# A graph layer on one core: edges on two column halves, carried sums and a row table in place of accumulating scatters

## The chip, the cores and the metric

The kernel runs on one core of one Trainium2 chip. The metric is the device time of one launch in microseconds (us); the time before is the median of six runs, 5170.73 us (5166.9 to 5174.27). A profile of one further execution goes with it.

## What is computed

One layer over 10000 nodes of 512 features and 160000 edges, all in float32. With xn = layernorm(x):

```python
h   = xn @ W
agg = segment_sum(h[src] * edge_weight[:, None], dst, 10000)   # dst is sorted
x   = x + relu(agg + bias) + mix(xn)        # mix: linear attention of 8 heads, then a norm
x   = x + ffn(layernorm(x))                 # 6 experts, one weighted mixture for all nodes
```

The kernel sums the gathered rows of xn first and multiplies by W afterwards, which is the same sum. `dst` is drawn so that low nodes have many edges and high nodes about eight.

## The kernel before

Rows are worked on in 20 chunks of 512 nodes (the last 272), four sub-rows a partition. Five stages follow one another.

**A** (lines 150 to 158): a chunk is loaded, normalised on VectorE with a power on GpSimd (lines 122 to 130, 126), and stored to `xn_d`. At the same time ten stores (line 209) fill the 10240 rows of `acc_d` with zeros.

**B** (lines 251 to 294): for each chunk transposes, the key product `pk`, exp, transposes and the context product `pc`. **C** (lines 297 to 365): for each chunk the query product `pq`, softmax, transposes, the output product `po` and a norm.

The **edges** are worked off during B and C. They lie in 1250 tiles of 128 edges, in order of `dst`. Six tiles (BATCH) make a step, 209 steps in all. For each tile an indirect DMA issued by GpSimd gathers 128 rows of `xn_d` into a buffer `msg` (line 217; a pool of 3 x BATCH = 18 buffers). VectorE makes a mask `sel` for the step (lines 221 and 224): for each edge a row of 128 columns (WIN) with its weight in the column of its node, counted from the step's first node. TensorE adds up the six products mask x rows in one PSUM tile of 128 nodes (line 229), ScalarE copies it out (line 231), and an indirect DMA with addition scatters its 128 rows into `acc_d` (line 232). Neighbouring steps can share nodes, so the scatters follow one another.

Lines 372 to 417 count the edges outside their step's 128 nodes; only if there are any does a loop over all tiles work them off one at a time.

**D** (lines 439 to 457): chunks of `acc_d` are loaded by SyncE's queue (line 441), transposed, multiplied by W, and the layer's first half is finished; GpSimd keeps a running sum `xsum` (line 457). **E** (from line 553): the feed-forward part, 256 products of 128x512 a chunk in two groups (lines 567 and 576).

Each engine works through its own list in order. A planner makes these lists from its own estimate of durations, so the order on an engine is not that of the text: pieces of a step's products stand between the products of B and C, 1 to 6 at a time in B and up to 31 in a row in C. The calls that spread the edges over B and C are these:

```python
for c, (_, r) in enumerate(chunks):
    edges_until((c - LEAD) / (2 * NCH - LEAD))          # B, line 254
...
    edges_until((NCH + c - LEAD) / (2 * NCH - LEAD))    # C, line 330
```

Of the kernel before, what the change touches and what calls it, by code (L numbers as in the profile page):

```python
# [8 lines left out]
F32 = mybir.dt.float32  # L9
I32 = mybir.dt.int32  # L10
AF = mybir.ActivationFunctionType
ALU = mybir.AluOpType
AX = mybir.AxisListType
# [3 lines left out]
P = 128  # L17
SUB = 4
EPS = 1e-5
HEAD = 64  # L20
QSCALE = HEAD ** -0.5
BATCH = 6
WIN = 128
PARTITIONS_OF_6 = [
    (6,), (5, 1), (4, 2), (4, 1, 1), (3, 3), (3, 2, 1), (3, 1, 1, 1),
    (2, 2, 2), (2, 2, 1, 1), (2, 1, 1, 1, 1), (1, 1, 1, 1, 1, 1),
# [4 lines left out]
def gps_layer_kernel(  # L31
# [19 lines left out]
    nc = tc.nc  # L51
    N, D = x.shape
    NET = src.shape[1]
# [18 lines left out]
    def tokens(t, c):  # L72
        b, r = chunks[c]
        return t[b : b + r * SUB, :].rearrange("(p s) d -> p s d", s=SUB)
# [14 lines left out]
    iota_w = const.tile([P, WIN], F32, name="iota_w")  # L89
    nc.gpsimd.iota(iota_w, pattern=[[1, WIN]], base=0, channel_multiplier=0,  # L90
                   allow_small_or_imprecise_dtypes=True)
    pid = const.tile([P, 1], F32, name="pid")
    nc.gpsimd.iota(pid, pattern=[[0, 1]], base=0, channel_multiplier=1,
                   allow_small_or_imprecise_dtypes=True)

    earlier = const.tile([P, P], F32, name="earlier")
# [7 lines left out]
    nc.scalar.dma_start(bias_b, gnn_bias.to_broadcast([P, D]))  # L104
    gamma_b = const.tile([P, D], F32, name="gamma_b")
    nc.scalar.dma_start(gamma_b, gamma.to_broadcast([P, D]))
    stats2 = const.tile([P, NCH, SUB, 2], F32, name="stats2")


# [2 lines left out]
    y_d = [dram.tile([r, SUB, D], F32, name=f"y_d{c}") for c, (_, r) in enumerate(chunks)]  # L112
    x1_d = [dram.tile([r, SUB, D], F32, name=f"x1_d{c}") for c, (_, r) in enumerate(chunks)]

    ACC_ROWS = -(-(N + P) // (8 * P)) * 8 * P
    acc_d = dram.tile([ACC_ROWS, D], F32, name="acc_d")

    def row_stats(t, r, mv):

# [41 lines left out]
    with ExitStack() as ph:  # L161
# [16 lines left out]
        nc.sync.dma_start(wq, w_qkv_t[:, :D].rearrange("(k p) d -> p k d", p=P))  # L178
        wo = wp.tile([P, KB, D], F32, name="wo")
        nc.sync.dma_start(wo, w_out_t.rearrange("(k p) d -> p k d", p=P))  # L180
        NB = -(-NET // BATCH)
        full = NET // BATCH
        base = ep.tile([P, NB], F32, name="base")
        idx = ep.tile([P, NB], I32, name="idx")
        place = ep.tile([P, NET], F32, name="place")
        tmp_ctx = ph.enter_context(ExitStack())
        tmp = tmp_ctx.enter_context(tc.tile_pool(name="edge_t", bufs=1))
        row_sb = tmp.tile([P, NET], I32, name="row_sb")
        nc.sync.dma_start(row_sb, dst[0:1, :].to_broadcast([P, NET]))

        nc.vector.tensor_copy(base[:, :full], row_sb[:, : full * BATCH].rearrange(
            "p (b j) -> p b j", j=BATCH)[:, :, 0])
        if NB > full:
            nc.vector.tensor_copy(base[:, full:], row_sb[:, full * BATCH : full * BATCH + 1])
        tmp_ctx.close()
        nc.vector.tensor_scalar(idx, base, pid, None, op0=ALU.add)

        nc.vector.tensor_copy(place, dst_sb)
        nc.vector.tensor_tensor(
            place[:, : full * BATCH].rearrange("p (b j) -> p b j", j=BATCH),  # L200
            place[:, : full * BATCH].rearrange("p (b j) -> p b j", j=BATCH),
            base[:, :full, None].to_broadcast([P, full, BATCH]), ALU.subtract)
        if NB > full:
            nc.vector.tensor_scalar(place[:, full * BATCH :], place[:, full * BATCH :],
                                    base[:, full : full + 1], None, op0=ALU.subtract)

        view = acc_d.rearrange("(b p) d -> p b d", p=P)
        for b in range(0, ACC_ROWS // P, 8):
            nc.scalar.dma_start(view[:, b : b + 8, :], zero[:, None, :].to_broadcast([P, 8, D]))

        def edges(b):

            t0 = b * BATCH
            n = min(BATCH, NET - t0)
            m = [mp.tile([P, D], F32, name="msg") for _ in range(n)]
            for j in range(n):
                nc.gpsimd.indirect_dma_start(  # L217
                    out=m[j], out_offset=None, in_=xn_d,
                    in_offset=bass.IndirectOffsetOnAxis(ap=src_sb[:, t0 + j : t0 + j + 1], axis=0))
            sel = ew.tile([P, BATCH, WIN], F32, name="sel")  # L220
            nc.vector.tensor_tensor(  # L221
                sel[:, :n, :], iota_w[:, None, :].to_broadcast([P, n, WIN]),
                place[:, t0 : t0 + n, None].to_broadcast([P, n, WIN]), ALU.is_equal)
            nc.vector.tensor_tensor(  # L224
                sel[:, :n, :], sel[:, :n, :],
                w_sb[:, t0 : t0 + n, None].to_broadcast([P, n, WIN]), ALU.mult)
            pm = psum_e.tile([P, D], F32, name="pm")
            for j in range(n):
                nc.tensor.matmul(pm, sel[:, j, :], m[j], start=j == 0, stop=j == n - 1)  # L229
            part = ew.tile([P, D], F32, name="part")  # L230
            nc.scalar.copy(part, pm)  # L231
            nc.gpsimd.indirect_dma_start(  # L232
                out=acc_d, out_offset=bass.IndirectOffsetOnAxis(ap=idx[:, b : b + 1], axis=0),
                in_=part, in_offset=None, compute_op=ALU.add)

        done = [0]

        def edges_until(share):
            stop = NB if share >= 1 else int(NB * share)
            while done[0] < stop:  # L240
                edges(done[0])
                done[0] += 1
# [54 lines left out]
        with ExitStack() as pb:  # L297
# [30 lines left out]
            for c, (_, r) in enumerate(chunks):  # L328
# [31 lines left out]
                for s in range(SUB):  # L360
# [2 lines left out]
                    nc.vector.scalar_tensor_tensor(ot[:r, s, :], ot[:r, s, :], mv[:r, s, 1:2],  # L363
                                                   xt[:r, s, :], op0=ALU.mult, op1=ALU.add)
                nc.sync.dma_start(y_d[c], ot[:r])
            edges_until(1)

        with ExitStack() as pb:  # L370
            fp = pb.enter_context(tc.tile_pool(name="far", bufs=1))
            inside = fp.tile([P, NET], F32, name="inside")
            nc.vector.tensor_scalar(inside, place, 0.0, None, op0=ALU.is_ge)
            w_far = fp.tile([P, NET], F32, name="w_far")
            nc.vector.scalar_tensor_tensor(w_far, place, float(WIN), inside, op0=ALU.is_lt, op1=ALU.mult)
            n_in = fp.tile([P, 1], F32, name="n_in")
            nc.vector.tensor_reduce(n_in, w_far, axis=AX.X, op=ALU.add)
            nc.vector.tensor_scalar(w_far, w_far, 0.0, None, op0=ALU.is_equal)
            nc.vector.tensor_tensor(w_far, w_far, w_sb, ALU.mult)
            pn = psum.tile([1, 1], F32, name="pn", tag="ps")  # L380
            nc.tensor.matmul(pn, n_in, ones, start=True, stop=True)
            n_far = fp.tile([1, 1], I32, name="n_far")
            nc.vector.tensor_scalar(n_far, pn, -1.0, float(NET * P), op0=ALU.mult, op1=ALU.add)
            any_far = nc.values_load(n_far[0:1, 0:1], min_val=0, max_val=NET * P)
            with tc.If(any_far > 0):
                with tc.For_i(0, NET) as t:
                    cs = fp.tile([P, 1], I32, name="cs")
                    nc.vector.tensor_copy(cs, src_sb[:, bass.ds(t, 1)])
                    cd = fp.tile([P, 1], F32, name="cd")
                    nc.vector.tensor_copy(cd, dst_sb[:, bass.ds(t, 1)])  # L390
                    cw = fp.tile([P, 1], F32, name="cw")
                    nc.vector.tensor_copy(cw, w_far[:, bass.ds(t, 1)])
                    m = fp.tile([P, D], F32, name="m_far")
                    nc.gpsimd.indirect_dma_start(
                        out=m, out_offset=None, in_=xn_d,
# [10 lines left out]
                    off = fp.tile([P, 1], F32, name="off")  # L406
                    nc.vector.tensor_scalar(off, cd, spare, None, op0=ALU.subtract)
                    nc.vector.scalar_tensor_tensor(off, seen, 0.0, off, op0=ALU.is_equal, op1=ALU.mult)
                    to = fp.tile([P, 1], I32, name="to")
                    nc.vector.tensor_scalar(to, off, spare, None, op0=ALU.add)  # L410
                    pm = psum.tile([P, D], F32, name="pm_far", tag="ps")
                    nc.tensor.matmul(pm, sel, m, start=True, stop=True)
                    part = fp.tile([P, D], F32, name="part_far")
                    nc.vector.tensor_copy(part, pm)
                    nc.gpsimd.indirect_dma_start(
                        out=acc_d, out_offset=bass.IndirectOffsetOnAxis(ap=to, axis=0),
                        in_=part, in_offset=None, compute_op=ALU.add)


# [16 lines left out]
    with ExitStack() as ph:  # L436
        io = ph.enter_context(tc.tile_pool(name="d_io", bufs=2))
        psum = ph.enter_context(tc.tile_pool(name="d_ps", bufs=3, space=PSUM))
        for c, (_, r) in enumerate(chunks):
            at = io.tile([P, SUB, D], F32, name="at")  # L440
            nc.sync.dma_start(at[:r], tokens(acc_d, c))
            yt = io.tile([P, SUB, D], F32, name="yt")
            nc.sync.dma_start(yt[:r], y_d[c])
            aT = io.tile([P, KB, SUB * P], F32, name="aT")
            transposed(aT, at, r, psum, "pt")
            gt = io.tile([P, SUB, D], F32, name="gt")
            for s in range(SUB):
                po = psum.tile([P, D], F32, name="po")
                times(po, aT, s, r, wg)
                nc.vector.tensor_tensor(gt[:r, s, :], po[:r, :], bias_b[:r], ALU.add)  # L450
            nc.vector.scalar_tensor_tensor(yt[:r], gt[:r], 0.0, yt[:r], op0=ALU.max, op1=ALU.add)
            nc.scalar.dma_start(x1_d[c], yt[:r])
            mv = stats2[:, c]
            row_stats(yt, r, mv)
            xn = io.tile([P, SUB, D], F32, name="xn")
            normalize(xn, yt, r, mv)
            nc.gpsimd.tensor_tensor(xsum[:r], xsum[:r], xn[:r], ALU.add)  # L457
# [164 lines left out]
```

## Time and profile before

| what | us |
|---|---|
| median of six runs | 5170.73 |
| the profiled execution | 5162.64 |
| its span | 5160.9 |
| stage A, until the first product | 0 to 176 |
| stages B and C, with the edges | 176 to 2557 |
| gap, until the first transposes of D | 2557 to 2582 |
| stage D | 2582 to 2913 |
| stage E | 2913 to 5161 |

PE (TensorE) is busy 4867.9 us of the span, DVE (VectorE) 1474.3, ACT (ScalarE) 627.5, POOL (GpSimd) 1897.7. A float32 matrix product is two records in the profile, each with its own weight load (PEld). The records of PE overlap, so the pace is read from start to start or from the length of a group in the chain, not from the mean length of a record. Stretches are us from the span's start.

### The profile page before, as it was taken

How to read it: one execution, taken by the hardware profiler on the slowest of the kernel's cores; microseconds unless marked ns; L12 is line 12 of the kernel's file. 1: busy time of each engine (PE TensorE's matmuls, PEld its weight loads, DVE VectorE, ACT ScalarE, POOL GpSimd, SP SyncE). 2: the span in 40 equal slices, each digit the busy share in tenths (PEclk: the TensorE clock that was granted, in tenths of full speed). 3: DMA queues.
4: the chain of work that ended last, by engine and by line, in shares of the span. 5: the costliest groups of instructions: out<-in, count | busy, mean ns of one | idle time of the engine just before them, and what ended most of it. 6: DMA issues, size and time to landing. Idle time of an engine off the chain costs nothing. (4 is left out here: it accounts for less than half of the span.)

```text
span 5160.9 us, 33449 instructions
## 1 busy us (share of the span) xinstructions
PE 4867.9 (94%) x12542; PEld 2220.1 (43%) x12542; DVE 1474.3 (29%) x2527; ACT 627.5 (12%) x1135; POOL 1897.7 (37%) x1613
## 2 busy tenths in 40 slices
PE   0699999999999999999799899999999999999999
PEld 0344444444444444444344344444444444444444
DVE  6333333333555555455466500000000000000000
ACT  0111111111111111111100111001111000111100
POOL 1544677777677777777633300000000000000000
PEclk9999999999999999999899999999999999999999
DMA  9855777777777777777675200000000000000000
GB/s 409 287 159 158 198 204 203 207 204 188 232 213 216 215 216 218 214 221 197 160 263 202 95 17 17 17 17 29 20 17 17 17 17 17 33 17 17 13 9 13
DMA packets 181719, 668.21 MB, mean 129 GB/s; under 512 B 28296, under 2 KB 29320, under 8 KB 151692
## 3 DMA queue, kind: packets, MB, share of 16 engines
q0 software_dynamic: 130096, 382.56, 28.6%
q1 hardware_dynamic: 28416, 192.13, 9.8%
q10 hardware_dynamic: 23044, 91.36, 4.4%
q8 instruction: 99, 1.62, 0.1%
q14 instruction: 64, 0.52, 0.0%
HBM read 487.79 MB, written 178.16 MB: 129 GB/s over the span
## 5 line engine op out<-in xcount | busy, mean ns | idle before, releaser
L217 POOL DMA_INDIRECT msg<-xn_d,src_sb x1250 | 1290.5, 1032 | 671.2 <-PE pm L229 329.1
L229 PE MATMUL pm<-msg,sel 128*128 128x512 f32 x2500 | 1132.8, 597 | 225.3 <-DMA msg<-xn_d,src_sb 222.7
L576 PE MATMUL po<-w_sb,hf 128*128 128x512 f32 (+2 forms) x2560 | 1102.3, 592 | 0.0
L567 PE MATMUL ph<-xnT,w_sb 128*128 128x512 f32 (+2 forms) x2560 | 1079.6, 583 | 0.0
L229 PEld LDWEIGHTS pm<-msg,sel 128*128 128x128 f32 x2500 | 460.7, 191 | 779.2 <-issue 664.8
L561 POOL TENSOR_TENSOR xt<-xt,b_b 128x2048 f32<-128x2048 f32 (+1 forms) x20 | 90.0, 4504 | 1857.3 <-DVE xn L130 1827.6
L576 PEld LDWEIGHTS po<-w_sb,hf 128*128 128x128 f32 (+2 forms) x2560 | 480.3, 188 | 618.3 <-issue 618.2
L567 PEld LDWEIGHTS ph<-xnT,w_sb 128*128 128x128 f32 (+1 forms) x2560 | 485.3, 190 | 578.5 <-issue 573.3
L578 DVE TENSOR_TENSOR xt<-xt,po 128x512 f32<-128x512 f32 (+1 forms) x80 | 55.0, 688 | 1962.9 <-PE po L576 1071.4
L232 POOL DMA_INDIRECT acc_d<-part,idx x209 | 355.0, 1698 | 88.2 <-issue 61.6
L570 ACT ACTIVATE hf<-ph,b_sb 128x512 f32<-128x512 f32 (+1 forms) x320 | 216.6, 677 | 867.4 <-PE ph L567 867.4
L221 DVE TENSOR_TENSOR sel<-iota_w,place 128x768 f32<-128x768 f32 (+1 forms) x209 | 199.2, 953 | 367.3 <-PE pm L229 365.9
L288 PE MATMUL pc<-xn,ktok 128*128 128x512 f32 (+1 forms) x640 | 293.5, 601 | 0.0
L146 PE MATMUL pq<-wq,xnT 128*128 128x512 f32 (+1 forms) x640 | 288.7, 611 | 0.0
L265 PE MATMUL pk<-xnT,wkv 128*128 128x512 f32 (+1 forms) x640 | 282.9, 584 | 0.0
L146 PE MATMUL po<-wg,aT 128*128 128x512 f32 (+1 forms) x640 | 279.0, 594 | 0.0
L146 PE MATMUL po<-mix,qT 128*128 128x512 f32 (+1 forms) x640 | 277.9, 592 | 0.0
L231 ACT COPY part<-pm 128x512 f32<-128x512 f32 x209 | 122.1, 584 | 788.8 <-PE pm L229 784.2
L224 DVE TENSOR_TENSOR sel<-sel,w_sb 128x768 f32<-128x768 f32 (+1 forms) x209 | 200.6, 960 | 5.2
L146 PEld LDWEIGHTS pq<-wq,xnT 128*128 128x128 f32 (+1 forms) x640 | 124.1, 194 | 162.8 <-issue 161.1
L288 PEld LDWEIGHTS pc<-xn,ktok 128*128 128x128 f32 (+1 forms) x640 | 116.7, 190 | 166.0 <-issue 115.8
L140 ACT COPY xnT<-pt 128x512 f32<-128x512 f32 (+1 forms) x80 | 46.0, 576 | 1157.9 <-PE pt L138 1157.9
(143 smaller groups left out, 2306.7 us busy)
## 6 DMA issues: line engine op xcount, KB each, us to landing
xt<-in_x SPq DMA_DIRECT2D x38, 1024.0 KB, 8.2
acc_d<-zero ACTq DMA_DIRECT2D x10, 2048.0 KB
msg<-xn_d,src_sb POOLq DMA_INDIRECT x1250, 3.9
xn_d<-xt ACTq DMA_DIRECT2D x19, 1024.0 KB, 20.4
xn<-xn_d SPq DMA_DIRECT2D x19, 1024.0 KB, 14.8
xnT_d<-xnT ACTq DMA_DIRECT2D x19, 1024.0 KB, 6.5
xnT<-xnT_d SPq DMA_DIRECT2D x19, 1024.0 KB, 5.7
y_d<-ot SPq DMA_DIRECT2D x19, 1024.0 KB, 5.8
```

What stands on the lines that cost most here:

```text
L146: nc.tensor.matmul(po[:r, :], t[:, kb, s * r : (s + 1) * r], w[:, kb, :], start=kb == 0, stop=kb == KB - 1)
L217: nc.gpsimd.indirect_dma_start(out=m[j], out_offset=None, in_=xn_d, in_offset=bass.IndirectOffsetOnAxis(ap=src_sb[:, t0 + j : t0 + j + 1], ...
L221: nc.vector.tensor_tensor(sel[:, :n, :], iota_w[:, None, :].to_broadcast([P, n, WIN]), place[:, t0 : t0 + n, None].to_broadcast([P, n, WIN ...
L224: nc.vector.tensor_tensor(sel[:, :n, :], sel[:, :n, :], w_sb[:, t0 : t0 + n, None].to_broadcast([P, n, WIN]), ALU.mult)
L229: nc.tensor.matmul(pm, sel[:, j, :], m[j], start=j == 0, stop=j == n - 1)
L231: nc.scalar.copy(part, pm)
L232: nc.gpsimd.indirect_dma_start(out=acc_d, out_offset=bass.IndirectOffsetOnAxis(ap=idx[:, b : b + 1], axis=0), in_=part, in_offset=None, co ...
L265: nc.tensor.matmul(pk[:, :n], wkv[:, kb, cb * P : (cb + 1) * P], xnT[:, kb, :n], start=kb == 0, stop=kb == KB - 1)
L288: nc.tensor.matmul(pc, ktok[:r, s, :], xn[:r, s, :], start=s == 0, stop=s == SUB - 1)
L567: nc.tensor.matmul(ph1[:m, :n], w1_sb[:, kb, f * P : f * P + m], xnT[:, kb, :n], start=kb == 0, stop=kb == KB - 1)
L570: nc.scalar.activation(hf[:m, :n], ph1[:m, :n], AF.Gelu, bias=b1_sb[:m, f : f + 1])
L576: nc.tensor.matmul(po[:r, :], hT[f][:m, s * r : (s + 1) * r], w2_sb[:m, f, :], start=f == 0, stop=f == NF - 1)
```

## The change

A step now works on two streams of edges at once. The 1250 tiles are split into a first and a second half of 625; a step takes three tiles (BATCH) of each, still six in all, and a range of 64 nodes (WIN) in each. A mask has 64 columns; the products of the first stream go to PSUM partitions 0 to 63, those of the second to 64 to 127, in turn. There are again 209 steps. The pool of `msg` buffers still has 3 x BATCH, which are now 9.

Instead of scattering with addition, each step adds to its own sums those of the step before, moved by the distance of the two ranges: one product of full width with a mask `shift` (0 or 1, made by VectorE) and the copy `part` of the step before. The finished rows are stored plainly by ScalarE's queue to `part_d`, 128 rows a step. The last step that contains a node thus holds its whole sum. The zero fill falls away but for 256 rows. One scatter with addition is left, at the end, for the nodes on the border of the two streams.

Stage D finds its rows by a table `row_of`: for each of the 80 sub-rows, VectorE compares the nodes with the ranges' starts in two passes over 418 columns and six small operations (`find_rows`). D then gathers each sub-row with an indirect DMA of GpSimd, 80 in all, in place of 20 plain loads by SyncE's queue. The test for edges outside the ranges covers the new conditions; the loop behind it works off all edges if it is entered.

```diff
-BATCH = 6
-WIN = 128
+BATCH = 3
+WIN = 64
+FAR = 1.0e5
...
+    part_d = dram.tile([DUMP_ROW + P, D], F32, name="part_d")
+    nc.scalar.dma_start(part_d[ZERO_ROW : ZERO_ROW + P, :], zero)
+    nc.scalar.dma_start(part_d[DUMP_ROW : DUMP_ROW + P, :], zero)
...
-        for b in range(0, ACC_ROWS // P, 8):
-            nc.scalar.dma_start(view[:, b : b + 8, :], zero[:, None, :].to_broadcast([P, 8, D]))
...
+        def find_rows(o, nodes):
+            past = ew.tile([P, 2 * NW], F32, name="past")
+            at = ew.tile([P, 2], F32, name="at")
+            nc.vector.scalar_tensor_tensor(past, flat, nodes, jump, op0=ALU.is_le, op1=ALU.mult,
+                                           accum_out=at[:, 0:1])
+            nc.vector.scalar_tensor_tensor(past, flat, nodes, climb, op0=ALU.is_le, op1=ALU.mult,
+                                           accum_out=at[:, 1:2])
...
+            for j in range(BATCH):
+                for h in range(2):
+                    if j < len(tiles[h]):
+                        t = tiles[h][j]
+                        m[h, j] = mp.tile([P, D], F32, name="msg")
+                        nc.gpsimd.indirect_dma_start(
+                            out=m[h, j], out_offset=None, in_=xn_d,
+                            in_offset=bass.IndirectOffsetOnAxis(ap=src_sb[:, t : t + 1], axis=0))
...
+            if i:
+                shift = ew.tile([P, P], F32, name="shift")
+                nc.vector.tensor_scalar(shift, step_w, step[:, i - 1 : i], None, op0=ALU.is_equal)
             pm = psum_e.tile([P, D], F32, name="pm")
-            for j in range(n):
-                nc.tensor.matmul(pm, sel[:, j, :], m[j], start=j == 0, stop=j == n - 1)
+            for j in range(BATCH):
+                for h in range(2):
+                    if j < max(1, len(tiles[h])):
+                        row = m[h, j] if (h, j) in m else m[0, 0]
+                        nc.tensor.matmul(pm[h * WIN : (h + 1) * WIN, :], sel[:, h, j, :], row,
+                                         start=j == 0, stop=i == 0 and j == max(1, len(tiles[h])) - 1,
+                                         skip_group_check=True)
+            if i:
+                nc.tensor.matmul(pm, shift, before_part[0], start=False, stop=True, skip_group_check=True)
             part = ew.tile([P, D], F32, name="part")
             nc.scalar.copy(part, pm)
-            nc.gpsimd.indirect_dma_start(
-                out=acc_d, out_offset=bass.IndirectOffsetOnAxis(ap=idx[:, b : b + 1], axis=0),
-                in_=part, in_offset=None, compute_op=ALU.add)
+            nc.scalar.dma_start(part_d[i * P : (i + 1) * P, :], part)
+            before_part[0] = part
...
+                for s in range(SUB):
+                    find_rows(row_of[:, c, s : s + 1], node[:, c, s : s + 1])
...
-            nc.sync.dma_start(at[:r], tokens(acc_d, c))
+            for s in range(SUB):
+                nc.gpsimd.indirect_dma_start(
+                    out=at[:r, s, :], out_offset=None, in_=part_d,
+                    in_offset=bass.IndirectOffsetOnAxis(ap=row_of[:r, c, s : s + 1], axis=0))
```

## The prediction

> **What bounds the kernel now.** I read the table of windows first, then the groups of instructions, the waits of PE, and two stretches of the timeline. Five stages follow one another: A (0 to 176 us, layer norm and its stores), B (176 to 1305, the first half of the mix with edges in between), C (1305 to 2557, the second half with edges), a gap of 25 us, then D (GNN product) and E (the feed-forward part). The columns are stretch, its length, busy time of PE, PEld, DVE, ACT and POOL with counts, PE clock, DMA share, GB/s.
>
> ```profile
> 10.00:140.00 130.00, 0.00 (x0) 0.00 (x0) 86.24 (x241) 0.00 (x0) 19.15 (x19) 1.00 1.01 417
> 176.00:1305.00 1129.00, 1128.98 (x3131) 530.45 (x3132) 377.13 (x603) 176.97 (x417) 743.70 (x676) 1.00 0.72 197
> 1305.00:2557.00 1252.00, 1195.51 (x2952) 528.00 (x2950) 651.23 (x1008) 184.37 (x313) 911.56 (x795) 0.99 0.74 211
> 2557.00:2582.00 25.00, 0.00 (x0) 0.00 (x0) 0.00 (x0) 0.58 (x1) 13.12 (x44) 0.50 0.51 130
> ```
>
> Stage A has no PE work and full DMA engines (1.01 at 417 GB/s). Stage B is PE without a hole. Stage C is PE with 56 us of holes; its POOL is busy 912 of 1252 us. So A is bound by bytes, B by PE, C by PE with POOL close behind. The groups say what the edges cost:
>
> ```profile
> L217 POOL DMA_INDIRECT msg<-xn_d,src_sb x1250 | 1290.5, 1032 | 671.2 <-PE pm L229 329.1
> L229 PE MATMUL pm<-msg,sel 128*128 128x512 f32 x2500 | 1132.8, 597 | 225.3 <-DMA msg<-xn_d,src_sb 222.7
> L232 POOL DMA_INDIRECT acc_d<-part,idx x209 | 355.0, 1698 | 88.2 <-issue 61.6
> ```
>
> Each of the 1250 products is two records (x2500). 597 ns is a record's length, not the pace: in the chain that ended last (start, length, what) 128 records take 54.94 us, 429.2 ns each with nothing between them,
>
> ```profile
> 3045.12 54.94 PE ph L567 x128
> 3100.06 54.96 PE po L576 x128
> ```
>
> and 429.5 with the small gaps, so a product costs 859 ns and all edges 2500 x 0.4295 = 1074 us. Of the 225 us of idle time 176 are the start; PE's waits after 390 us show what is left for late gathers:
>
> ```profile
> PE pm L229 <- DMA msg<-xn_d,src_sb: 46.9, 39, 3.2
> ```
>
> Where they come from is seen in C, where one chunk has 25 to 31 products in one run. There PE uses a gather every 0.86 us, POOL gives one every 1.25 us or more (0.95 busy, 0.30 before it) with a scatter of 1.6 us in between, and only the 18 buffers filled ahead hide it:
>
> ```profile
> 1917.13 3.67 PE L229 MATMUL pm<-msg,sel 128*128 128x512 f32 x8 [0.37 <-DMA msg<-xn_d,src_sb]
> 1921.07 1.13 PE L229 MATMUL pm<-msg,sel 128*128 128x512 f32 x2 [0.27 <-DMA msg<-xn_d,src_sb]
> 1925.04 1.59 PE L229 MATMUL pm<-msg,sel 128*128 128x512 f32 x2 [2.85 <-DMA msg<-xn_d,src_sb]
> ```
>
> ```profile
> 1918.88 1.61 POOL L232 DMA_INDIRECT acc_d<-part,idx  x1 [0.30 <-issue]
> 1920.80 0.99 POOL L217 DMA_INDIRECT msg<-xn_d,src_sb  x1 [0.30 <-PE pm L229]
> 1922.10 0.96 POOL L217 DMA_INDIRECT msg<-xn_d,src_sb  x1 [0.30 <-issue]
> 1923.36 0.95 POOL L217 DMA_INDIRECT msg<-xn_d,src_sb  x1 [0.30 <-issue]
> ```
>
> **1. Products on halves (B and C).** The 1250 products now fill 64 columns each, taking turns between the halves, so two may run side by side. The trace of before holds no pair of halves; the bounds are full turns (859 ns each, nothing gained) and full pairs (429.5 ns each, -537 us). I take a value between. Records start in program order in every row, and a product is two records that need the same half: the second record of one product can run beside the first of the next, no more. So n products in a run take n + 1 steps of 429.5 ns instead of 2n. In the order of the changed kernel as built, the 1250 products stand in 420 runs (235 in B with 577 products, 185 in C with 673), since the planner puts pieces of 1 to 6 between other products. That makes (1250 + 420) x 0.4295 = 717 us: **-357 us**.
>
> The Trainium skill ("TensorE: Matmul & The Clock Gate", Part 3, packing small matmuls) reports 2.38 times for three column tiles and says matmuls start and end in program order; an estimate by its ratio (0.79 per tile) would be 1074 / 1.59 = 676 us. No row here shows either.
>
> **2. The shift product.** 208 products of the full width at 859 ns: **+179 us**, on PE's path like all else there. Each waits for the copy of the sum before (584 ns on ACT, line 231), which is done long before, except between runs in C, where 3 us of products lie in between.
>
> **3. Changing the array's shape.** Runs of halves stand between full-width work, 839 changes. The nearest rows are small products on part of the array:
>
> ```profile
> 2930.84 0.19 PE L531 MATMUL pe<-ones,e_row 1*6 1x1 f32 x2
> 2930.96 1.13 PE L567 MATMUL ph<-xnT,w_sb 128*128 128x512 f32 x2
> 2932.01 0.38 PE L536 MATMUL ps<-e_col,owner 6*128 6x1 f32 x2
> ```
>
> Two full records from 2930.96 to 2932.01 take 1.05 us instead of 0.86: 0.1 us for each of the two changes around them. Bounds 0 and 0.1; I take 0.075, since a run's last record may hide part: **+63 us** (0 to 84).
>
> On this the skill ("TensorEngine Tiling (Array Packing)", Key Properties) speaks against the change: it says that a change of the tiling mode drains the engine, without a figure. The row agrees with a small price.
>
> **4. Gathers (C).** This is the hidden edit: message buffers are 3 x BATCH, so 18 become 9, while a step still gathers six. A chunk with six steps has, after its 16 po products, 29 products in 8 runs, five shifts and three pq products: (29 + 8) x 0.43 + 4.3 + 2.6 + 16 x 0.075 = 24.0 us of PE work. Nine gathers are there; the other 20 start at 1.2 us (first buffer free), come every 1.3 us (1.25 in the rows; 1.33 is the mean with 0.30) and land 3.9 us after issue: 1.2 + 19 x 1.3 + 3.9 = 29.8, plus 1.3 for POOL's pow of line 126 and 1.7 for the last product and shift: 32.8. So PE stands 8.8 us per chunk; with five steps 23 products give 25 against 20, 5 us. 13 x 8.8 + 6 x 5 = 144; with the 1.2 to 1.67 us issues in the rows I take 165. Before it was 47: **+118 us** (60 to 150). The scatters leave POOL (-355 us busy) and their bytes come back as plain stores on ACT's queue; ACT is busy 184 of 1252 us and has room for 209 issues of about 0.5 us (rows of ACT's queue: 0.33 to 0.47). In B one gather is wanted every 1.9 us, so nine buffers do.
>
> B and C together: -357 + 179 + 63 + 118 = **+3 us**.
>
> **5. Stage A.** Ten stores of zeros, 20.97 MB, go; at 417 GB/s they are 50 us of full DMA engines. What is late next is DVE: a chunk of statistics and normalising comes every 5.1 us in the timeline, 20 x 5.1 + 7 = 109, then the last store, the index loads and the first gather, about 20: 129 against 176. **-47 us** (-25 to -52).
>
> **6. Row table and DVE.** 81 searches, two passes over 128x418 and six over 128x1. From 128x512 at 0.75 us and 128x1250 at 1.45 a pass is 0.6; a 128x1 row (L270) is 0.16: 2.2 us busy, 1.6 with the overlap of neighbours. The built order puts 20 into each of the first four chunks of B: 32 to 44 us beside 16 that are there, against 48 us of PE. Bounds 0 and 4 x 12; **+10 us**. The masks cost less (two passes over 768 were 1.92 us a step; four over 192 are about 1.4, the shift mask 0.25).
>
> **7. Gap and stage D.** Before, three scatters of about 5.5 us follow one another in the gap; now one store and one scatter, then four row gathers of 1.25 us and landing: **-5 us** (-10 to +10). In D POOL gets 80 gathers, 5 us a chunk beside 5.5 that it has, in a chunk of 15.8 us of PE, and the order keeps them three chunks ahead of the sums: nothing, though 3 to 5 us a chunk if that cover went.
>
> **Sum:** +3 - 47 + 10 - 5 = -39 on the profiled execution's 5162.6 us (span 5160.9), which is 8 us under the median of 5170.7. On the median: 5132, **forecast 5130 us**.
>
> **Rivals.** *The halves take turns* (slower). If the array serves one half at a time, step 1 gives nothing: +179 + 63, and the gathers keep up (33 us of PE work in the burst), -37. 205 - 47 + 10 - 5 = +163: **5334 us**. For it: no row shows an overlap, every record in the trace follows its neighbour at 0.43 us. Against: nothing in the rows excludes it either. Each tenth of the overlap is worth 20 us, so it decides below about 0.8 of it. *Switches are free and gathers meet 1.25 us* (faster): -178, stalls 150 instead of 47, A -47, gap -5: **5045 us**. *Overlap, but gathers at 1.5 us* since all bytes of C now fall into the bursts: 20 x 0.2 x 19 = +76: **5210 us**. *It does not do what it says*: the fallback for ranges over 64 nodes would add 1250 dependent steps of many us; with at most 51 nodes from one range's start to the next in these inputs I give it nothing.
>
> **How the numbers follow.** Forecast case 0.47 (0.36 faster, 0.06 same, 0.05 slower; 5075 to 5185 by its bounds), turns 0.35, free switches 0.10, slow gathers 0.08. Faster 0.46, slower 0.48, within 0.2% (10 us, about what a measurement of this kernel can tell) 0.06. The range 5060 to 5360 leaves out the fast end of the third case and the slow end of the second; it spans both signs because step 1 has no row.
>
> **What would show it.** In the profile after: records of products with 64 columns starting 0.43 us apart or less with overlapping ends (step 1) or a product every 0.86 (turns); PE's wait for msg in C at 100 to 200 us; first product near 130 us; POOL without scatters; the first four chunks of B no longer than 50 us each. I would be wrong by a wide margin if the pair overlaps fully, or if a change of shape costs much more than 0.1 us.

## The result, and the profile after

The changed kernel takes **5180.8 us** (median of 16 runs, 5177.24 to 5187.83), the kernel before 5169.9 beside it (36 runs, 5162.33 to 5178.2): 1.0022 times, 95% interval 1.0016 to 1.0029. It is 11 us slower; the forecast was 5130. The profiled execution took 5183.34 us with a span of 5181.6, 20.7 more than the span before, and the steps below are held against that. (The two profiled executions lie 7 us under and 3 us over the medians of their kernels, so about 10 of the 20.7 are spread.)

The table of windows of the changed kernel, B and C (columns as in the prediction):

```profile
147.00:1247.00 1100.00, 1087.39 (x3229) 417.91 (x3228) 448.53 (x1657) 176.97 (x412) 545.66 (x561) 1.00 0.62 192
1271.00:2573.00 1302.00, 1163.03 (x3175) 417.14 (x3174) 595.28 (x1339) 182.03 (x312) 683.56 (x688) 0.93 0.63 204
```

Each stage is counted here from its first product to its last: B from 143 to 1247 us (before, 176 to 1281), C from 1271 to 2573 (before, 1305 to 2554); some 25 us of other products lie between. B, 1104 us long, is as long as before (1105); C takes 1302 us instead of 1249. C's PE has 139 us of holes, against 54 before, and a granted clock of 0.93 instead of 0.99. POOL is 228 us less busy in it, since the scatters have left, but C is no shorter for that. The groups of products, then PE's waits (total, times, longest):

```profile
L276 POOL DMA_INDIRECT msg<-xn_d,src_sb x1250 | 1232.6, 986 | 1189.8 <-PE pm L300 870.6
L300 PE MATMUL pm<-msg,sel 128*64 128x512 f32 x2500 | 833.9, 640 | 290.6 <-DMA msg<-xn_d,src_sb 146.8
L304 PE MATMUL pm<-part,shift 128*128 128x512 f32 x416 | 238.5, 656 | 0.0
```

```profile
PE pm L300 <- DMA msg<-xn_d,src_sb: 146.8, 76, 8.4
PE pt L161 <- DMA at<-part_d,row_of: 24.1, 4, 18.1
```

The 2500 records of the edges keep PE busy 833.9 us instead of 1132.8, so halves do run side by side. The waits for late gathers are 146.8 us where 46.9 were; POOL in turn waits 870.6 us for PE, for a free buffer. Whose fault it is can't be read from either line alone.

How the halves run is seen in the timeline of PE in C (start, length, records):

```profile
1930.13 0.74 PE L161 MATMUL pt<-ident,qt 128*128 128x128 f32 x5 [0.23 <-DVE qt L423]
1930.80 2.80 PE L300 MATMUL pm<-msg,sel 128*64 128x512 f32 x12
1933.52 1.12 PE L304 MATMUL pm<-part,shift 128*128 128x512 f32 x2
1934.48 0.60 PE L161 MATMUL pt<-ident,qt 128*128 128x128 f32 x4
1935.01 1.07 PE L300 MATMUL pm<-msg,sel 128*64 128x512 f32 x2
1936.02 4.56 PE L169 MATMUL po<-mix,qT 128*128 128x512 f32 x10
```

Six products (12 records) take 2.72 us from start to start, three products' time and 0.145 more: **pairs overlap fully**, each record of one half beside a record of the other (7 ns apart in the single records). A lone product (x2) takes 1.01 us, the changes of shape around it included, and leaves the other half empty. Around each run the single records show the price of a change of shape: the last full record before it lasts 523 ns to the next start instead of 429.5 and the first pair 480, **0.144 us into halves**; behind it the last pair lasts 523 and the first full record behind 533 (a transpose 165 instead of 109), **0.197 us out** (0.15 before a transpose). In and out make 0.341 us for a run.

And this is a stall, in the same view and in the table of windows:

```profile
1891.90 1.13 PE L304 MATMUL pm<-part,shift 128*128 128x512 f32 x2
1893.45 1.04 PE L300 MATMUL pm<-msg,sel 128*64 128x512 f32 x2 [0.42 <-DMA msg<-xn_d,src_sb]
1896.63 1.07 PE L300 MATMUL pm<-msg,sel 128*64 128x512 f32 x2 [2.14 <-DMA msg<-xn_d,src_sb]
1901.46 4.28 PE L300 MATMUL pm<-msg,sel 128*64 128x512 f32 x8 [3.75 <-DMA msg<-xn_d,src_sb]
1905.67 1.12 PE L304 MATMUL pm<-part,shift 128*128 128x512 f32 x2
```

```profile
1890.00:1896.80 6.80, 4.24 (x11) 0.98 (x9) 4.53 (x13) 0.59 (x1) 5.28 (x6) 1.00 0.82 272
1897.00:1898.50 1.50, 0.71 (x2) 0.00 (x0) 0.00 (x0) 0.00 (x0) 1.20 (x2) 1.00 0.98 404
1896.80:1901.10 4.30, 0.91 (x2) 0.02 (x1) 0.00 (x0) 0.00 (x0) 3.39 (x4) 0.70 0.97 392
1901.10:1905.30 4.20, 3.84 (x8) 1.39 (x8) 0.00 (x0) 0.00 (x0) 3.19 (x4) 0.50 1.03 404
```

It costs three times. PE stands (2.14, then 3.75 us). Products whose neighbour's rows have not landed run alone (x2 in 1.04 us). And after the long wait the granted clock is 0.50: eight records take 4.28 us where twelve took 2.80. Call a slot the 0.859 us in which the array does one product or one pair. Over C the edge and shift records take 242 us more than their slots and changes: 139 of it idle, 52 lost at half the clock (PE works 104 us of C at it), and by difference 51 in products that ran alone (358 records start with no other within 0.13 us, where the order alone makes 86). Before, the like was 68 us: 54 idle and 14 at half the clock. The Trainium skill ("TensorE: Matmul & The Clock Gate", Part 1) says that an idle window of about 3.4 us throttles the array to half rate and that as long a busy stretch releases it. The trace agrees on the release: full clock is back at 1905.4, after 3.9 us of records at 0.50. It agrees less on the start: the rows show 1.00 until 1898.5 and a mean of 0.70 up to 1901.1, so the clock fell near 1898.5, only 0.8 us into the wait of 3.75 us, after 2.14 us of wait and 1.07 of work.

The long wait seems to have a reason other than the number of buffers; it stays with 16 of them (e14 below). SyncE's queue issues a 1 MB store of `y_d` and a 1 MB load of `in_x`, and the gather that PE then waits for is issued 0.44 us behind the store:

```profile
1892.01 0.32 SPq L439 DMA_DIRECT2D y_d<-ot  x1
1892.42 0.38 SPq L408 DMA_DIRECT2D xt<-in_x  x1
1892.46 1.43 POOL L276 DMA_INDIRECT msg<-xn_d,src_sb  x1 [0.31 <-issue]
```

That gather lands 9.0 us after its issue; the median in C is 4.4. The DMA engines are at 0.97 to 1.03 meanwhile. All 19 waits of more than 2.5 us before edge products in C end with such a gather, 0.44 us behind a store of `y_d` and landing 8.7 to 13.0 us after its issue; they make 82 of the 134 us that PE stands there. In the kernel before PE waits for 12 such gathers too (8.6 to 11.7 us to landing), but only 3.2 us for one and at most 1.0 for each of the others. No run moves these transfers, so this reason is read from the trace and not tested.

### The profile page after: what moved, and what is told of

It reads as the page before. It is cut to its first block, busy times and chain, and to the rows that moved or that the text cites. A ratio compares the mean times of both kernels' runs of the same rounds, so it can differ in the third digit from the quotient of the medians.

```text
span 5181.6 us, 35867 instructions
## 1 busy us (share of the span) xinstructions
PE 4824.5 (93%) x12958; PEld 2008.1 (39%) x12958; DVE 1504.3 (29%) x3983; ACT 628.2 (12%) x1135; POOL 1583.5 (31%) x1492
## 5 line engine op out<-in xcount | busy, mean ns | idle before, releaser
L276 POOL DMA_INDIRECT msg<-xn_d,src_sb x1250 | 1232.6, 986 | 1189.8 <-PE pm L300 870.6
L300 PE MATMUL pm<-msg,sel 128*64 128x512 f32 x2500 | 833.9, 640 | 290.6 <-DMA msg<-xn_d,src_sb 146.8
L300 PEld LDWEIGHTS pm<-msg,sel 128*64 128x64 f32 x2500 | 197.0, 140 | 785.6 <-issue 356.7
L284 DVE TENSOR_TENSOR sel<-iota_w,place 128x192 f32<-128x192 f32 x418 | 131.8, 354 | 495.0 <-PE pm L300 494.7
L304 PE MATMUL pm<-part,shift 128*128 128x512 f32 x416 | 238.5, 656 | 0.0
L169 PEld LDWEIGHTS po<-mix,qT 128*128 128x128 f32 (+1 forms) x640 | 118.5, 188 | 161.1 <-issue 135.8
```

The lines of the kernel that those rows point to most:

```text
L169: nc.tensor.matmul(po[:r, :], t[:, kb, s * r : (s + 1) * r], w[:, kb, :], start=kb == 0, stop=kb == KB - 1)
L276: nc.gpsimd.indirect_dma_start(out=m[h, j], out_offset=None, in_=xn_d, in_offset=bass.IndirectOffsetOnAxis(ap=src_sb[:, t : t + 1], axis=0))
L284: nc.vector.tensor_tensor(sel[:, h, :n, :], iota_w[:, None, :].to_broadcast([P, n, WIN]), place[:, t0 : t0 + n, None].to_broadcast([P, n, ...
L300: nc.tensor.matmul(pm[h * WIN : (h + 1) * WIN, :], sel[:, h, j, :], row, start=j == 0, stop=i == 0 and j == max(1, len(tiles[h])) - 1, ski ...
L304: nc.tensor.matmul(pm, shift, before_part[0], start=False, stop=True, skip_group_check=True)
```

## The experiments

Theory 1: the loss sits in C, in gathers that nine buffers can't fetch ahead. Theory 2: the array eats the gain, by changes of shape and half-empty slots. A ratio stands against the kernel before, timed beside it. The kernel before took 5285 to 5291 us beside e1 to e4, e9 to e12, e17 and e18, but 5162 to 5170 beside the others, so runs are compared in us within a group, and where two groups are compared the text says so.

| run | us | ratio, 95% interval |
|---|---|---|
| e1 16 buffers | 5256.4 | 0.9945 (0.9929 to 0.9962) |
| e2 whole steps | 5137.0 | 0.9716 (0.9683 to 0.9749) |
| e3 halves in turn | 5156.8 | 0.9747 (0.9718 to 0.9775) |
| e4 full width | 5311.1 | 1.0046 (1.0029 to 1.0064) |
| e5 the changed kernel | 5185.9 | 1.0031 (1.0018 to 1.0043) |
| e6 spread steps | 4893.9 | 0.9469 (0.9454 to 0.9485) |
| e7 no row table | 5172.8 | 1.0008 (0.9998 to 1.0017) |
| e8 zero fill back | 5217.2 | 1.0098 (1.0081 to 1.0115) |
| e9 before, spread | 5223.8 | 0.9869 (0.9837 to 0.9900) |
| e10 spread, full width | 5386.0 | 1.0172 (1.0138 to 1.0206) |
| e11 spread, shift in the middle | 5106.1 | 0.9647 (0.9614 to 0.9680) |
| e12 spread, 9 buffers | 5180.8 | 0.9789 (0.9757 to 0.9820) |
| e13 the changed kernel | 5179.3 | 1.0030 (1.0017 to 1.0042) |
| e14 16 buffers | 5062.2 | 0.9802 (0.9789 to 0.9816) |
| e15 spread steps | 4895.2 | 0.9480 (0.9467 to 0.9493) |
| e16 spread, shift in the middle | 4946.2 | 0.9580 (0.9567 to 0.9593) |
| e17 before, spread | 5225.9 | 0.9887 (0.9848 to 0.9926) |
| e18 spread, no short waits | 4993.4 | 0.9437 (0.9398 to 0.9476) |

**Buffers (e1, e13, e14).** One line:

```diff
-        mp = ph.enter_context(tc.tile_pool(name="edge_m", bufs=3 * BATCH))
+        mp = ph.enter_context(tc.tile_pool(name="edge_m", bufs=16))
```

Expected of e1:

> The changed kernel with 16 message buffers in place of 9, nothing else. Theory 1 (the gathers): between 1271 and 2573 us the changed kernel's PE stands 139 us, nearly all for late gathers, against 54 us before, and the records behind a stall run at half the pace. With 16 buffers the two weigh about as before: 85 us of idle time and some 40 of slow records go, about 5055 us. Theory 2 (the array): the gain is eaten by the 839 changes of shape and the half-empty slots, and a stall only moves; 5170 to 5185 us.

Expected of e13:

> The changed kernel, beside the three that follow. 1.0022 to 1.0031 times the kernel before so far.

Expected of e14:

> The changed kernel with 16 message buffers, nothing else. If the buffers are the cause of the stalls in C (139 us of idle time, some 40 of slow records, against 54 and 14 before): 100 to 130 us less than the changed kernel. If it is the bunching, where 30 products in a row use gathers at twice the pace at which they come: 16 buffers are empty as well after half of a burst, so 30 to 60 us less.

e1 had no changed kernel beside it, hence e13 and e14: 5179.3 against 5062.2, **117 us** for one number, and the kernel is then 2% faster than before. Not all of it is waiting: with 16 buffers the planner also makes another order in C, with 371 runs of halves instead of 420, and 49 x 0.341 = 17 us of changes of shape go with them. PE's idle time in B and C falls by 65 us; the rest, some 35, is mostly pairs that meet again. Windows of e14, B and C, and its wait:

```profile
147.00:1222.00 1075.00, 1074.89 (x3227) 415.99 (x3226) 448.17 (x1656) 177.07 (x412) 552.75 (x568) 1.00 0.63 198
1246.00:2449.00 1203.00, 1112.48 (x3173) 414.05 (x3172) 597.38 (x1338) 182.24 (x312) 680.35 (x681) 0.95 0.67 220
```

```profile
PE pm L300 <- DMA msg<-xn_d,src_sb: 85.8, 24, 6.8
```

B has no hole left and C is 99 us shorter, but its PE still stands 91 us and its clock is 0.95. By the sum over C that gave 242 us for the changed kernel, 160 are left, against 68 before: the buffers take 82 of the 174 us. What they take are the short waits: 18 waits of 3.9 to 6.8 us stay, 79 us together, and each ends with a gather issued 0.44 us behind a 1 MB store of `y_d`, as above. Theory 1 holds for about half of the loss; the rest stands behind gathers that land late.

**Whole steps (e2, e3, e4).** With 16 buffers (as in all runs below, where nothing else is said), the six products of a step and its shift follow one another: the first is the one whose rows come last, and the planner is told to place the others as soon as they can go.

```diff
+            seq = [(h, j) for j in reversed(range(BATCH)) for h in range(2) if j < max(1, len(tiles[h]))]
+            with ExitStack() as rush:
+                for k, (h, j) in enumerate(seq):
+                    if k == 1:
+                        rush.enter_context(tc.high_priority())
...
```

Expected of e2:

> 16 buffers, and the six products of a step and its shift product stand together on PE (209 runs of six instead of 420 runs of one to six). Theory 2: a change into halves costs 0.144 us and one out of them 0.197 us in the trace, so 211 runs fewer save 72 us, and 731 slots of 0.859 us become 625, 91 us less: about 160 us under the kernel with 16 buffers, more if the gathers never stall: 4760 to 4900 us. Theory 1 alone: equal to the kernel with 16 buffers within 20 us, since the products then wait for the gathers of a whole step.

119 us less than e1, where 160 or more were expected. The planner drew 163 of the 209 steps into B, where PE then stood 208 us, about half of it for copies and exponentials that other work had covered before.

e3: `for h in (1, 0) for j in reversed(range(BATCH))` in the list.

Expected of e3:

> As the one before, but a step issues its three products of the second stream first and then the three of the first. If two products run beside each other only where they are neighbours in the list, only the third and fourth do, and a step takes 5 slots instead of 3: 209 x 2 x 0.859 = 359 us more than whole steps in alternation. If each half takes its products from a queue of its own, 0 to 60 us more.

20 us more than e2: the second answer in its number, but by way of e2's holes. The timeline shows how:

```profile
702.47 2.36 PE L344 MATMUL pk<-xnT,wkv 128*128 128x512 f32 x4
704.77 3.70 PE L303 MATMUL pm<-msg,sel 128*64 128x512 f32 x12
708.40 1.12 PE L308 MATMUL pm<-part,shift 128*128 128x512 f32 x2
```

The twelve records take 3.63 us from start to start, against 2.72 in alternation and 5.15 one by one. The single records start alone twice, then in four pairs, then alone twice: the first record of the second half, seventh in the list, starts beside the third. A half takes work past the other's waiting records, but not from far. What that costs, 0.91 us in each of 209 steps, went for the most part into e2's holes: PE's idle time in B is 101 us in e3, 208 in e2.

e4 has masks of 128 columns, zeros in the other stream's half, and 14 buffers:

Expected of e4:

> Whole steps again, but each mask has 128 columns, zeros in the half of the other stream, so products neither pair nor change the array's shape (14 buffers instead of 16, and mask operations twice as wide). It prices the whole use of halves: 625 x 0.859 = 537 us more for the products, 209 x 0.341 = 71 us less for the changes, 466 us above whole steps. If pairing were worth nothing (the halves take turns) it would be 71 us faster than whole steps.

174 us more than e2, not 466: e2 isn't bound by PE, so it can't price PE's work. That called for an order without holes.

**Spread steps (e6, e15; e5 beside e6).** Whole steps, and the first product held behind the PE instruction that stands before it in the text, with the steps spread over the chunk; the three calls stand behind each pk in B, each pq and each po in C:

```diff
+                    if k == 0:
+                        tc.keep_in_program_order(ins)
...
+                    edges_until((c + (cb + 1) / KB) / (2 * NCH))
...
+                    edges_until((NCH + c + (s + 1) / (2 * SUB)) / (2 * NCH))
...
+                    edges_until((NCH + c + 0.5 + (s + 1) / (2 * SUB)) / (2 * NCH))
```

Expected of e5:

> The changed kernel itself, on the same chip as the three that follow, so that they can be compared with it. By its first measurement 1.0022 times the kernel before.

Expected of e6:

> 16 buffers, whole steps, and each step held behind a fixed product of the mix (one after each pk in B, after each pq and each po in C), so that about five steps a chunk lie evenly. Theory 2 (what counts is the array): 625 slots and 208 shifts of 0.859 us, 209 runs at 0.341 us and 1219 us of other work, 2008 us for B and C against 2429 in the changed kernel: 421 us less, about 4760 us or a ratio of 0.92, if no gather is late: 31 gathers of 1.25 us fit into a chunk of 50 us. Theory 1 alone (gathers bound it as a whole): 1250 x 1.25 = 1563 us are no bound here either, so it also says faster, but with stalls left wherever POOL's other work or a bulk transfer comes between: 4850 to 4950 us.

Expected of e15:

> The spread steps again, 0.947 times the kernel before so far. The rest of the stalls, and the wins of whole pairs (731 slots to 625, 91 us) and of fewer changes (420 runs to 209, 72 us) lie between the kernel with 16 buffers and this one: 163 us and the stalls that 16 buffers leave.

292 us under the changed kernel (e5), 167 under 16 buffers (e14); 5.2% under the kernel before. Windows of e15, B and C:

```profile
140.00:1237.00 1097.00, 1033.06 (x3390) 424.94 (x3390) 467.41 (x1730) 180.42 (x422) 620.50 (x637) 1.00 0.68 214
1254.00:2288.00 1034.00, 995.88 (x3062) 390.08 (x3062) 573.34 (x1298) 180.15 (x305) 634.10 (x631) 0.98 0.72 241
```

C, 1302 us in the changed kernel, is 1034; the wait for gathers is down to 1.1 us in e6. It missed the expected 4760 by 134 us: 63 are idle time in B, 58 of it short waits of `pc` for its copy, and 20 are the count at the end; the rest is open. The 4850 to 4950 us that theory 1 gave are met in number only, since the stalls on which they rested aren't there.

**The kernel before in the same order (e9, e17).** The order might have made that gain by itself.

Expected of e9:

> The kernel before (full width, 18 buffers, scatters) with the same order as the spread steps: six products together, one step at each of the same places. It asks how much of the 276 us between the spread version and the kernel before is the order and how much the change. By the sum B and C are 1219 us of other work and 1250 x 0.859 = 1074 us of products, 2293 us against 2380: about 5085 us, with up to 60 us more for the short waits of pc that the spread version shows too. If the order alone made the gain: about 4895 us.

Expected of e17:

> The kernel before in the order of the spread steps, again 0.987 times the kernel before as in its first run, about 5095 us. If it is 0.948 as the spread version was, the order alone made the gain.

Not so: 5224 and 5226 us, 0.987 and 0.989 of the kernel before beside them, and more than the 5162 us that it takes beside e15. e9 misses its expected 5085 by 139 us; about 100 are idle time of PE in B and C, the rest is open. PE doesn't wait for gathers in it either; windows of e17:

```profile
176.00:1440.00 1264.00, 1178.90 (x3184) 552.48 (x3184) 392.11 (x608) 178.98 (x421) 803.85 (x741) 1.00 0.70 188
1459.00:2617.00 1158.00, 1137.95 (x2852) 516.18 (x2852) 634.35 (x980) 180.67 (x305) 828.82 (x732) 0.99 0.75 213
```

Held against e15 (another group, but neither waits for gathers), halves take 291 us off these two stretches (1264 + 1158 - 1097 - 1034). 21 of them are shorter waits in B, and C has 18 more of waits with the count at its end, so 288 are PE's work; the sum for whole pairs is 625 x 0.859 - 208 x 0.859 - 209 x 0.341 = 287.

**Full width, spread (e10).**

Expected of e10:

> The spread steps with masks of 128 columns, zeros in the other stream's half (14 buffers): no pairs and no change of shape. PE is now what bounds B and C (1 us of waits for gathers left), so the sum should show whole: 625 x 0.859 = 537 us more for the products, 209 x 0.341 = 71 us less for the changes, about 5360 us. With 2 to 60 us more where 31 gathers no longer keep up or VectorE's wider masks are late.

B and C are 1358 and 1264 us, 491 more than e15's (another group again), with 19 us more idle in B: 472 against 466. Measured with no stall in the way, the sum of pairs and changes is right.

**Price of a change (e11, e16).** The shift product stands after the first pair: the same slots, and more runs. The trace has 392, 183 more than e15's 209 and not 208, since 25 times the planner puts the last two pairs of a step right before the first pair of the next.

Expected of e11:

> The spread steps with the shift product after the first pair instead of after the third: the same products and slots, but 208 more runs of halves, so two more changes of shape a step. At the trace's 0.144 us into halves and 0.197 us out of them: 208 x 0.341 = 71 us more than the spread steps, about 4965 us. By the forecast's 0.075 a change: 31 us more. If changes of shape cost nothing: equal.

Expected of e16:

> The spread steps with 208 more runs of halves and nothing else changed. At 0.144 us into halves and 0.197 us out: 71 us more than the spread steps beside it. By the forecast's 0.075 us a change 31 us more. If the changes are hidden: equal.

e11 has no spread version beside it. e16 against e15: 51 us, 0.28 a run: 19.5 us in B for 79 runs (0.25, the short waits behind them hide part) and 31.7 in C for 104 (0.30). By the prices read from the single records the 183 runs, 93 of them before a transpose, cost 183 x 0.341 - 93 x 0.047 = 58 us; without the idle time PE takes 56 more. By the forecast's 0.075 a change it would be 27. The changes in the timeline of e16 stand as read above:

```profile
1506.41 1.08 PE L306 MATMUL pm<-msg,sel 128*64 128x512 f32 x4
1507.42 1.13 PE L303 MATMUL pm<-part,shift 128*128 128x512 f32 x2
1508.48 1.94 PE L306 MATMUL pm<-msg,sel 128*64 128x512 f32 x8
1510.35 1.86 PE L161 MATMUL pt<-ident,qt 128*128 128x128 f32 x15
```

A shift between two runs takes 1.06 us instead of 0.86, a run of two pairs 1.87 for 1.72.

**Nine buffers, spread (e12).**

Expected of e12:

> The spread steps with 9 message buffers instead of 16. If the number of buffers made the stalls of the changed kernel (forecast's step 4), stalls come back, 100 us or more. If it was the bunching of five or six steps in a row in C, nine buffers are nearly enough: three gathers wait ahead and the other three of a step are issued at 1.25 us and land 4.4 us later, about 8 us, where steps stand some 9.5 us apart: 0 to 40 us more than with 16.

I expected little. PE waits 138 us for gathers again. The kernel is at 0.979, against 0.948 for 16 buffers in another group; in its own, e11 has 16 buffers, 183 more runs of halves and 1.1 us of such waits, and takes 75 us less:

```profile
PE pm L303 <- DMA msg<-xn_d,src_sb: 138.0, 81, 6.4
```

Even steps some 10 us apart don't save nine buffers.

**Two small terms (e7, e8).** Both are the changed kernel with 9 buffers. e7 fills `row_of` from `node` in place of the searches, so it gathers other rows in D; e8 puts back the ten stores.

Expected of e7:

> The changed kernel without the 80 searches of the row table on VectorE; the node numbers themselves are taken as rows, so stage D gathers other rows. Forecast's term: 10 us less than the changed kernel, from the first four chunks of B (0 to 48). The trace shows these chunks 53 to 56 us long against 45 to 46 before, so 20 to 30 us less if the searches are the cause, 0 if it is the products there.

Expected of e8:

> The changed kernel with the ten stores of zeros put back at their old place, to a tensor that nobody reads. Prices the term of stage A alone: the first product came at 143.4 us against 175.8, so 32 us more than the changed kernel; 47 by the forecast; 0 if the earlier start came from something else.

Against e5: 13 us for the row table, 31 for the zero fill. Neither is the price of its term alone, since each edit also changed the planner's order. e7 has 374 runs of halves instead of 420, and 46 x 0.341 = 16 us are as much as it gains. Its chunks of B take 50.7 us instead of 52.1 even from the fifth on, where 8 runs a chunk stand in place of 12, and PE has no idle time in the first four chunks of e5, where the searches stand. So the 13 us are the price of the order, and nothing shows that the searches hold up PE. In e8 the first product comes at 177.6 us instead of 143.3, 34 later, and 45 fewer runs set off part of that.

**The last waits (e18).** `pc` one column block later, the count ahead of B.

Expected of e18:

> The spread steps with two waits taken out: the context product pc of a column block is issued after the key product of the next block instead of right behind the transposes and copy that it waits for (0.75 us each, 62 us of idle time in B), and the count of edges outside their range is made at the start of B instead of at its end (PE waits 20 us for it). By the sum 62 + 20 = about 80 us less than the spread version's 4895, so 4815 us; 4880 or more if other waits take their place.

0.944 with an interval that overlaps the spread steps' 0.948: no gain is shown. The waits of `pc` are gone, but the first transposes come at 151 instead of 140 us (the count stands on VectorE's path there), and PE waits 64 us for `qt`. That wait may come with the group: e11 has 53 us of it, e16, the same program in a faster group, 16. Whether the 80 us are there in the faster group is open.

## Why the prediction was wrong

The direction of the forecast failed: -39 us were summed, +20.7 came. Steps 1, 3 and 4 were wrong. The errors of 1 and 3, -89 and +76, nearly cancel, which is luck; those of 4 and 5, +56 and +15, turned the sign. By its steps, in us:

| step | forecast | measured | from |
|---|---|---|---|
| 1 products on halves | -357 | -446 | 731 slots of 0.859 for 1250 |
| 2 shift product | +179 | +179 | 208 slots |
| 3 changes of shape | +63 | +139 | 420 runs at 0.33; 104 to 128 by e16 |
| 4 gathers in C | +118 | +174 | 242 against 68 |
| B and C together | +3 | +51 | profile (steps 1 to 4 make +46) |
| 5 stage A | -47 | -32 | first product 143; e8: 31 |
| 6 row table | +10 | +13, within B | e7, with 46 fewer runs |
| 7 gap and D | -5 | +2 | profile |

**Step 1** failed in its rule, to the good: "the second record of one product can run beside the first of the next, no more". It rested on records that start in program order, as in every row of before. But the first record of the second product starts 7 ns behind that of the first, ahead of the first product's second record, and e3 has a record start beside one four places ahead of it. Two neighbours run fully beside each other, so a run of n products takes n/2 slots, rounded up, not n + 1 half slots. Neither the program order nor the ratio of 0.79 a tile that the forecast cites holds here.

**Step 3** was mis-sized. It took 0.075 us for each of 839 changes from a row where small products stand between full ones; single records give 0.144 and 0.197, and e16 bears them out. This ate the surplus of step 1.

**Step 4** had the edit (9 buffers) and the place right, and e14 confirms that the buffers cost: 117 us, of which 17 are fewer runs. Two of its terms failed. It let every gather "land 3.9 us after issue"; once a chunk one lands about 9 us after, behind a 1 MB store and load, and 82 of the 134 us of standing lie there. The rows of before held such gathers, but PE was slow enough to hide most of them. And it counted only the standing. That part even was below the forecast (139 - 54 = 85), so its size was partly luck; the clock at half rate after a stall (52 against 14) and products that lost their partner (51) came on top. Nothing in the old trace had shown the second, and its stalls of up to 3.2 us had set off little of the first.

**Step 5** took VectorE's pace for what is late next and had the first product at 129 us; it came at 143. VectorE ended its last normalising at 122.6 us instead of 109; the 20 us behind it were right. **Step 6** held in its number only: the first four chunks of B are 53 to 56 us long (its sign was 50 at most), but PE has hardly any idle time in them, and what e7 saves is about what its 46 fewer runs are worth. **Step 7:** the gap shrank by 10 us, from 28 to 18, but D grew by 12; 6 of these are waits for row gathers.

Of the rivals, *the halves take turns* is refuted by every pair, *free switches* by the single records. *Slow gathers*, 5210, was the nearest time. Its pace is refuted: gathers follow one another at 1.25 us, as before (median 1254 ns from start to start, 1271 before). Its reason, bytes that fall into the bursts, is seen in the one gather a chunk that lands late.

So pairs gave 446 us in B and C, and more than that went again: 179 to the carry, 139 to changes of shape, and 174 to late gathers, about half of these from a pool that shrank only because its size is written as a multiple of BATCH. With 16 buffers the change gives 2%, with whole, evenly placed steps 5.2%.

## What to carry to other kernels

When a constant is halved, look for every pool whose size is written with it: the work in flight is halved too. Price a stall by what follows it, not by its length alone: here a clock at half rate and pairs that no longer meet cost as much again. Look at what a burst of gathers meets: here one a chunk landed behind two bulk transfers, and evenly spread steps did not wait for it. Where a planner makes the order, count the runs again after every edit: e7, e8, e14 and e16 each changed more than the line that was edited. Work on parts of the array pays when pairs stand together in long runs, so give the scheduler whole pieces and fixed places for them.

## What the runs showed of the hardware

- Two float32 products of 64 columns on the two halves take 0.859 us together, the time of one; the starts lie 7 ns apart.
- A half isn't held up by the other's records that stand before its own: the seventh record started beside the third, four places ahead (e3).
- A change of the array's shape cost 0.144 us into halves and 0.197 us out of them, 0.15 before a transpose. The Trainium skill ("TensorEngine Tiling (Array Packing)", Key Properties) tells of the drain; these are its numbers here.
- In a wait of 3.75 us the granted clock fell to 0.50 after 0.8 us and stayed there for the first 3.9 us of work behind the wait.
- A gather issued 0.44 us behind a 1 MB store, with a 1 MB load beside it, landed about 9 us after its issue; the median in C was 4.4 us.
- The same kernel before took 5162 us beside one group of runs and 5291 beside another. In e1, beside 5289, VectorE stood 58.7 us before `qm` for a releaser that the trace doesn't name; in e14, the same program beside 5162, it has no such wait. The record's number of the chip doesn't tell the groups apart: chip 7 stands beside 5289 (e1 to e4) and beside 5170 (e5 to e8). The cause is open.
